# Block exchanges that land on every fourth partition, in a transformer block with expert routing

## The chip, the cores and the metric

The kernel runs on one core of a Trainium2 chip. Its time is the device time of one execution in microseconds (us). Lower is better. It was run three times; the median is what a change is compared with.

## The reference

A transformer block on 16 sequences of 256 tokens, width 256, all in f32:

```python
shift = silu(t) @ W_ada.T + b_ada                  # per sequence
h = ln(x, ln1_g, ln1_b) + shift
qkv = (h @ Wqkv.T).reshape(b, n, 3, 16, 64)        # 16 heads of 64
q = ln(qkv[:, :, 0] per head, qn_g, qn_b)          # normalised over the head's 64 values
k = ln(qkv[:, :, 1] per head, kn_g, kn_b)
attn = softmax(q @ k.T / 8);  x = x + (attn @ v) @ Wout.T
gate = softmax(x @ Wgate.T)                        # 8 experts
vals, idx = top_k(gate.T, 512)                     # each expert takes its 512 best of 4096 tokens
y = (gelu(ln(x[idx]) @ fc1.T + b1) @ fc2.T + b2) * vals
x[idx] += y
```

## The kernel before, in words

**Attention, sequence by sequence.** A sequence's 256 tokens are two tiles (t) of 128. `First` normalises them and transposes them to `hT`. `Group(b, g, t)` multiplies one tile by 512 columns of the qkv weights (g 0 and 1 are queries, 2 and 3 keys, 4 and 5 values), so a group holds eight heads. For queries and keys ScalarE squares the result (L701), VectorE sums each head's 64 squares (L705), GpSimd takes the power -1/2 (L103), and VectorE scales the result into `qk` (L721). The mean over a head needs no instruction there, because the query and key weights are centred once at the start (`center`, L604 and L605). `Quad(b, d)` is four heads: two pairs i, each with two heads j. `scores` (L813) works on a pair with its two heads side by side in TensorE, `maxima` (L821) and `exps` (L830) make the exponentials `pr` and their sums, `normalise` (L841, GpSimd) divides, and `product` (L900) multiplies the transposed probabilities `prT` by the values. `Tail` projects (L926), adds the residual, normalises for the experts and makes the gate's logits.

**Two ways to transpose.** Queries, keys and probabilities have to be transposed, 128 by 128 and f32. For the sequences in `DIRECT` (0 and 15) TensorE does it against an identity matrix (L730 for q and k, L881 for probabilities), and ScalarE copies the result out of PSUM (L742, L888). For the other 14 sequences VectorE transposes inside 32x32 blocks (`turn`, L754 and L851), and an exchange through DRAM puts the blocks where they belong: one store of 512 KB (`away`, L761 and L859) and four loads of 128 KB (`back`, L773 and L873), load q writing the 32 partitions from 32q on. ScalarE then applies the gains to q and k (`affine`, L781 and L789). All these DMAs are issued by SyncE.

**The routing.** As soon as sequences 0 to 14 are done, a search over 30 bits finds for each expert the value of its 256th best gate. Every step is a compare and count on VectorE (L1091), a matmul that adds the counts (L1100) and a decision on VectorE (L1115), one after the other. Sequence 15's attention goes on beside it, and TensorE gets filler transposes (`fill`, L551) where it would sit idle. The routing's first instruction on TensorE is a transpose of the gates (L1028). After the search come a placement, a list of tokens and the first gathers.

**The experts.** Fifteen of the 16 jobs (eight experts, each once for the first 256 tokens and once for the rest) run in a plain loop of `up` (L1286), `gelu`, `down` (L1302) and a scatter, with the second routing's steps spread between them; the first job runs at the end of the planned part.

**What sets the order.** Each engine runs its instructions in the order in which they were issued. For the attention and the first routing, `at(...)` records 3863 steps, and the tuple `PLACES` gives each of them a place; the steps are issued sorted by place. So the order is a written list, and a change of steps needs another list.

Of the kernel before, what the change touches and what calls it, by code (L numbers as in the profile page):

```python
# [12 lines left out]
AF = mybir.ActivationFunctionType  # L13
ALU = mybir.AluOpType
AX = mybir.AxisListType
# [3 lines left out]
P = 128  # L19
# [45 lines left out]
def kernel(  # L65
# [83 lines left out]
    def make_others():  # L149
# [21 lines left out]
    DIRECT = (0, B - 1)  # L171
# [11 lines left out]
        0.3, 0, 3.3, 4.02, 3.75, 5.04, 4.42, 7.26, 0, 0, 8, 9.39, 21.59, 15.62, 11.2, 13.11,  # L183
        17.01, 18.4, 0, 0, 0, 0, 0, 0, 0, 3.5, 4.21, 5.54, 4.52, 5.23, 6.09, 6.6, 7.26, 10.88,
        12.83, 15.02, 15.97, 19.79, 26.15, 26.82, 14.6, 16.55, 20.39, 21.18, 23.31, 28.69, 29.8,
        16.33, 18.28, 20.99, 23.06, 25.36, 27.79, 28.46, 20.58, 22.53, 23.91, 24.94, 27, 28.24,
        29.13, 24.1, 26.05, 33.83, 36.09, 29.35, 31.3, 32.01, 32.8, 34.94, 36.73, 37.55, 31.08,
        33.03, 33.74, 34.68, 36.66, 53.28, 54.22, 37.45, 40.14, 40.85, 42.51, 44.49, 48.92, 51.33,
        39.18, 41.13, 41.84, 44.39, 46.57, 52.83, 53.55, 47.04, 49.88, 49.37, 52, 32.81, 35.54,
        36.58, 38.73, 40.91, 41.63, 34.34, 35.13, 39.64, 41.35, 42.12, 38.46, 43.11, 35.71, 37.26,  # L190
        38.22, 40.69, 41.79, 42.61, 37.86, 39.18, 41.6, 42.67, 44.05, 40.42, 46.02, 47.26, 44.13,
        45.37, 46.16, 50.43, 53.73, 55.38, 45.97, 48.92, 51.34, 54.17, 54.89, 50.16, 57, 45.15,
        47.17, 47.96, 53.16, 63.68, 68.13, 47.77, 50.37, 52.25, 64.12, 67.64, 51.61, 70.34, 71.58,
        55.11, 56.95, 58.1, 60.54, 66.44, 67.15, 56.35, 57.14, 59.63, 78.31, 81.13, 59.36, 83.25,
        56.13, 59.53, 64.4, 68.49, 77.87, 78.83, 58.15, 59.06, 67.58, 80.48, 81.62, 66.42, 84.27,
        86.99, 74.97, 76.5, 77.37, 83.28, 91.94, 92.75, 77.1, 79.32, 82.37, 90.48, 91.2, 80.91,
        94.7, 81.36, 83.07, 83.86, 89.48, 96.74, 97.55, 85.48, 87.48, 90.39, 94.26, 96.51, 89.21,
        101.81, 103.78, 115.15, 119.13, 120.28, 120.28, 121.51, 122.02, 123.82, 124.54, 127.81,
        128.58, 118.62, 122.45, 124.6, 123.6, 124.46, 125.96, 131.29, 132, 134.85, 135.67, 0,
        14.5, 15.21, 24.51, 12.59, 13.3, 22.98, 42.23, 43.1, 51.1, 53.05, 53.76, 54.55, 57.55,  # L200
        58.75, 60.22, 62.17, 62.88, 63.82, 65.82, 66.61, 58.34, 60.44, 61.15, 61.94, 63.92, 65.21,
        66.01, 67.37, 70.57, 72.17, 76.37, 61.95, 63.9, 64.61, 65.7, 67.68, 68.47, 69.27, 70.63,
        73.83, 75.43, 80.28, 64.71, 66.66, 68.61, 70.56, 66.88, 68.83, 69.54, 70.33, 72.31, 73.1,
        71.36, 73.46, 74.17, 74.96, 77.7, 78.49, 73.24, 75.19, 75.9, 76.84, 79.1, 80.3, 81.1,
        82.46, 85.66, 87.26, 91.69, 75.99, 78.33, 79.7, 80.49, 82.47, 83.67, 84.47, 85.83, 89.03,
        90.63, 95.66, 78.75, 82.11, 85.14, 88.44, 82.38, 84.88, 86.03, 87.54, 88.6, 84.28, 85.07,
        88.45, 89.51, 87.27, 90.63, 92.63, 95.83, 97.43, 106.44, 90.92, 92.16, 93.24, 96.03,
        97.14, 92.76, 94.2, 96.94, 98.95, 95.76, 99.75, 101.11, 104.31, 105.91, 111.23, 114.89,
        95.72, 97.75, 98.54, 105.78, 106.84, 98.35, 104.27, 106.69, 108.65, 105.51, 109.45,
        111.11, 114.31, 116.23, 129.4, 100.79, 102.03, 102.82, 107.6, 111.66, 102.63, 105.23,  # L210
        108.51, 112.87, 106.47, 113.67, 115.03, 118.46, 120.66, 130.42, 131.51, 107.46, 109.86,
        111.01, 118.96, 120.13, 109.26, 110.05, 114.35, 118.52, 114.08, 125.1, 127.2, 130.51,
        133.3, 141.66, 108.48, 111.06, 112.93, 115.26, 116.69, 110.46, 111.97, 116.17, 117.3,
        114.85, 118.1, 119.46, 123, 125.2, 140.64, 142.75, 112.25, 115.02, 115.88, 121.61, 127.2,
        114.25, 117.33, 122.52, 129.35, 121.34, 130.15, 132.1, 135.7, 138.5, 144.42, 124.04,
        125.39, 126.18, 128.68, 131.68, 125.99, 127.14, 129.59, 132.81, 128.41, 133.61, 135.3,
        138.5, 140.5, 145.44, 148.04, 162.09, 166.05, 167.29, 167.2, 168.45, 170.6, 176.27,
        177.75, 178.81, 179.57, 165.56, 169.54, 171.6, 170.69, 171.55, 172.1, 179.26, 182.41,
        182.94, 184.62, 0, 25.96, 26.82, 28.77, 24.84, 27.58, 28.44, 80.92, 82.6, 87.02, 88.97,
        90.12, 91.3, 93.36, 94.15, 88.75, 90.7, 91.41, 93.18, 95.16, 96.53, 92.53, 95.16, 95.93,  # L220
        97.85, 99.83, 101.03, 101.83, 103.19, 106.39, 109.11, 113.89, 97.33, 99.5, 100.43, 101.22,
        103.23, 104.02, 105.91, 107.91, 111.11, 112.71, 118.29, 99.06, 106.19, 109.35, 116.84,
        102.83, 107.18, 108.05, 109.42, 112.27, 117.91, 104.71, 106.68, 107.45, 111.3, 113.48,
        123.45, 113.27, 115.38, 116.09, 117.08, 120.74, 121.84, 122.64, 124, 127.2, 128.8, 135.66,
        122.09, 124.04, 124.79, 125.58, 127.81, 128.74, 129.54, 130.9, 134.1, 136.5, 140.7,
        125.93, 129.06, 131.66, 135.17, 125.06, 131.08, 132.3, 134.29, 135.83, 126.59, 128.1,
        135.2, 137.04, 134.02, 137.84, 142.5, 145.7, 147.3, 151.65, 128.38, 130.48, 133.26,
        139.13, 140.19, 133.42, 137.62, 140.04, 142, 138.86, 142.8, 144.16, 147.36, 149.3, 158.17,
        159.41, 133.83, 135.07, 136.66, 141.86, 150.58, 136.44, 138.58, 140.95, 149.36, 139.82,
        151.38, 153.33, 157.29, 160.13, 174.38, 142.53, 144.37, 145.16, 148.86, 159.5, 143.77,  # L230
        146.12, 149.77, 156.32, 148.59, 160.3, 162.13, 165.33, 166.93, 175.4, 177.26, 143.55,
        145.57, 147.08, 156.65, 163.01, 147.38, 151.38, 155.74, 162.23, 152.62, 163.81, 165.73,
        169, 171.33, 188.03, 152.67, 153.91, 154.7, 161.71, 163.62, 156.93, 157.72, 160.8, 164.83,
        159.33, 166.93, 168.93, 172.6, 174.2, 187.01, 190.56, 153.69, 155.11, 160.3, 164.02,
        172.48, 157.53, 161.26, 163.11, 173.09, 162.84, 177.27, 179.47, 183.07, 185.07, 192.51,
        159.19, 160.43, 164.77, 168.87, 178.44, 161.63, 163.81, 167.96, 173.7, 167.65, 179.24,
        180.67, 185.03, 188.27, 193.53, 194.62, 200.92, 204.76, 207.03, 205.96, 207.15, 209.49,
        214.68, 215.39, 217.95, 220.68, 209.17, 212.86, 214.51, 214.65, 215.68, 217.39, 219.42,
        220.01, 224.43, 225.43, 0, 29.62, 30.62, 42.89, 26.48, 29.1, 43.22, 133.39, 134.22,
        135.45, 139.54, 141.4, 142.77, 144.97, 146.17, 137.18, 140.04, 140.8, 144.65, 146.78,  # L240
        147.98, 138.91, 142.19, 142.9, 146.53, 148.76, 149.97, 150.77, 152.13, 155.33, 156.93,
        162.22, 148.19, 150.14, 151.19, 151.98, 154.51, 155.71, 156.93, 158.93, 162.13, 163.73,
        167.93, 146.31, 148.53, 156.44, 158.68, 149.92, 152.34, 153.05, 153.86, 158.73, 165.44,
        154.56, 156.66, 158.13, 158.92, 161.03, 168.93, 160.21, 163.22, 164.23, 165.02, 167.05,
        167.84, 168.64, 170.13, 174.2, 176.2, 181.41, 169.03, 170.98, 171.88, 172.67, 174.91,
        176.11, 176.91, 178.27, 181.47, 183.07, 187.27, 170.76, 172.71, 177.08, 179.96, 172.49,
        175.51, 176.3, 180.52, 181.58, 174.31, 175.1, 181.43, 182.49, 179.73, 184.67, 187.07,
        190.27, 191.87, 198.01, 173.51, 176.72, 180.45, 182.46, 185.39, 177.32, 179, 183.37,
        184.78, 182.19, 187.27, 190.27, 193.47, 195.07, 213.66, 214.9, 185.12, 187.85, 188.64,
        195.66, 196.89, 187.25, 189.6, 194.75, 196.28, 193.28, 198.67, 201.03, 207.89, 210.23,  # L250
        222.54, 186.14, 192.68, 193.47, 196.57, 198.1, 189.06, 191.55, 197.48, 198.71, 194.71,
        199.51, 202.23, 205.43, 207.03, 221.52, 223.68, 199.03, 200.27, 201.06, 205.05, 206.37,
        200.87, 202.02, 204.14, 205.76, 203.87, 207.53, 209.03, 217.89, 220.23, 228.22, 200.05,
        201.47, 202.98, 207.25, 208.71, 202.07, 204.94, 208.16, 209.93, 206.98, 210.73, 212.23,
# [1383 lines left out]
```

## Time and profile before

| | |
|---|---|
| Three runs | 1088.24, 1091.94, 1093.52 us (median 1091.94) |
| Profiled execution | 1091.3 us |
| Its span | 1089.5 us |
| Granted TensorE clock, mean | 0.993 |
| TensorE busy | 1050.4 us, 96% of the span |
| VectorE busy | 809.4 us, 74% |
| GpSimd busy | 617.5 us, 57% |
| ScalarE busy | 592.3 us, 54% |
| DMA | 238.56 MB, mean 219 GB/s |
| Exchange DMAs, issue to landing, median | stores 4.7 (probabilities) and 4.1 us (q, k); loads 4.0 to 4.1 us |

The profile is one execution, taken instruction by instruction. Its time is 1.8 us over its span. A row of a group gives line, engine, operation, output and inputs with their shapes, how often, then busy time, the mean duration of one in ns, and the idle time of the engine ahead of it with what ended that. An f32 matmul of the program is two records in the profile, a transpose is one. Busy time counts overlapping instructions once. The page's rows of digits show 40 equal slices of the span, each digit the busy share in tenths.

### The profile page before, as it was taken

What the parts mean: (1) busy time and instruction counts of PE and PEld (TensorE: products, weight loads), DVE (VectorE), ACT (ScalarE), POOL (GpSimd) and SP (SyncE); (2) the same over time, 40 slices, a digit from 0 to 9 for tenths busy, and PEclk for the clock granted to TensorE, in tenths of its full rate; (3) what the DMA queues carried; (4) which work ended last, traced back from release to release, by engine and by line L of the source; (5) the groups of instructions that cost most, each with busy time, mean ns of one, the idle gap of its engine ahead of it and who ended that gap; (6) DMA issues with size and microseconds to landing.
All of it is one profiled execution on the core that took longest, in us unless ns stands there. A gap on an engine that the chain in (4) does not pass through costs nothing. (4 is left out here: it accounts for less than half of the span.)

```text
span 1089.5 us, 18716 instructions
## 1 busy us (share of the span) xinstructions
PE 1050.4 (96%) x5611; PEld 686.6 (63%) x5611; DVE 809.4 (74%) x2257; ACT 592.3 (54%) x1656; POOL 617.5 (57%) x997
## 2 busy tenths in 40 slices
PE   6999999999999999999999999999988999999996
PEld 4555646555454655555565555656667888888885
DVE  6658888889788797898888887885678588655440
ACT  1768666666566665675666656675612322332331
POOL 3676776778667686667757666665501333333332
PEclk9999999999999999999999999999999999999998
DMA  6025899999999999998999999985130556655661
GB/s 214 1 78 165 269 276 304 291 281 257 283 292 280 280 299 290 289 280 263 277 299 286 265 302 265 321 260 164 61 102 20 149 161 199 186 171 163 192 203 20
DMA packets 167700, 238.56 MB, mean 219 GB/s; under 512 B 17328, under 2 KB 139440, under 8 KB 167600
## 3 DMA queue, kind: packets, MB, share of 16 engines
q1 hardware_dynamic: 159680, 227.08, 69.9%
q0 software_dynamic: 6144, 8.39, 4.2%
q10 hardware_dynamic: 1776, 1.90, 0.5%
q8 instruction: 45, 0.74, 0.3%
q14 instruction: 55, 0.45, 0.1%
HBM read 136.64 MB, written 100.66 MB: 218 GB/s over the span
## 5 line engine op out<-in xcount | busy, mean ns | idle before, releaser
L688 PE MATMUL pm<-wq,hT 128*128 128x512 f32 x768 | 362.1, 607 | 10.1 <-DVE qk L721 3.9
L841 POOL TENSOR_SCALAR pr<-pr,sums 128x256 f32<-128x256 f32 x512 | 237.6, 485 | 102.6 <-DVE sums L837 95.0
L830 ACT ACTIVATE pr<-sc,nmax 128x256 f32<-128x256 f32 x512 | 237.7, 482 | 92.3 <-DVE nmax L821 75.2
L688 PEld LDWEIGHTS pm<-wq,hT 128*128 128x128 f32 x768 | 137.1, 191 | 165.3 <-issue 131.3
L103 POOL TENSOR_TENSOR ss<-ss,neghalf 128x8 f32<-128x8 f32 x128 | 211.2, 1650 | 10.7
L821 DVE TENSOR_REDUCE nmax<-sc 128x2 f32<-128x512 f32 x256 | 165.3, 672 | 19.4 <-PE sc L813 19.1
L851 DVE STREAM_TRANSPOSE pb<-pr 128x512 f32<-128x512 f32 x224 | 150.0, 689 | 15.9 <-POOL pr L841 9.4
L813 PE MATMUL sc<-kT,qT 64*128 64x256 f32 x1024 | 136.8, 396 | 1.0 <-ACT kT L789 0.6
L701 ACT ACTIVATE sq<-pm 128x512 f32<-128x512 f32 x128 | 76.4, 605 | 102.5 <-PE pm L688 100.5
L900 PE MATMUL po<-prT,v 128*64 128x256 f32 x1024 | 129.0, 387 | 1.3 <-DMA prT<-blocks 1.3
L813 PEld LDWEIGHTS sc<-kT,qT 64*128 64x128 f32 x1024 | 91.3, 186 | 50.3 <-issue 28.9
L1319 POOL DMA_INDIRECT out<-y,idx x32 | 51.3, 1604 | 120.6 <-DVE y L1313 66.0
L1286 PE MATMUL ph<-xT,w 128*128 128x256 f32 x512 | 117.8, 383 | 0.0
L1302 PE MATMUL py<-w,hid 128*128 128x256 f32 x512 | 116.3, 380 | 0.0
L926 PE MATMUL pw<-wo,oT 128*128 128x256 f32 x512 | 115.3, 382 | 0.0
L926 PEld LDWEIGHTS pw<-wo,oT 128*128 128x128 f32 x512 | 96.2, 190 | 20.9 <-issue 6.0
L830 ACT ACTIVATION_READ_ACCUMULATOR pr<-sc,nmax 128x1 f32 x512 | 109.2, 213 | 0.0
L900 PEld LDWEIGHTS po<-prT,v 128*64 128x64 f32 x1024 | 66.5, 136 | 66.0 <-issue 20.1
L705 DVE TENSOR_REDUCE ss<-sq 128x8 f32<-128x512 f32 x128 | 85.0, 669 | 28.8 <-ACT sq L701 28.3
L1293 ACT ACTIVATE hid<-ph,vec 128x256 f32<-128x256 f32 x128 | 60.4, 474 | 84.4 <-PE ph L1286 79.4
L1302 PEld LDWEIGHTS py<-w,hid 128*128 128x128 f32 x512 | 95.6, 190 | 12.8
L1286 PEld LDWEIGHTS ph<-xT,w 128*128 128x128 f32 x512 | 95.4, 190 | 12.8
(141 smaller groups left out, 1098.3 us busy)
## 6 DMA issues: line engine op xcount, KB each, us to landing
blocks<-pb SPq DMA_DIRECT2D x112, 512.0 KB, 4.7
prT<-blocks SPq DMA_DIRECT2D x448, 128.0 KB, 4.1
kblocks<-kb SPq DMA_DIRECT2D x56, 512.0 KB, 4.1
w<-in_fc2T SPq DMA_DIRECT2D x16, 1024.0 KB, 5.8
w<-in_fc1T SPq DMA_DIRECT2D x16, 1024.0 KB, 8.3
qraw<-kblocks SPq DMA_DIRECT2D x112, 128.0 KB, 4.0
kT<-kblocks SPq DMA_DIRECT2D x112, 128.0 KB, 4.1
out<-tok SPq DMA_DIRECT2D x32, 128.0 KB, 3.9
```

What stands on the lines that cost most here:

```text
L103: nc.gpsimd.tensor_tensor(dst, src, neghalf[:, : src.shape[1]], ALU.pow)
L688: nc.tensor.matmul(self.pm, hTs[self.b][:, c, bass.ts(self.t, P)], wq[:, c, bass.ts(self.g, GW)], start=(c == 0), stop=(c == DC - 1),)
L705: nc.vector.tensor_reduce(self.ss[:, 0, :], self.sq.rearrange("p (h d) -> p h d", d=HD), AX.X, ALU.add,)
L813: nc.tensor.matmul(self.sc[i, j][:, t, :], qTs[self.b][rows, hp, bass.ts(t, P)], keys[rows, hp] if direct else keys[rows, hp // 4, hp % 4] ...
L821: nc.vector.tensor_reduce(self.nmax[i, j], self.sc[i, j], AX.X, ALU.max, negate=True)
L830: nc.scalar.activation(self.pr[i, j][:, t, :], self.sc[i, j][:, t, :], AF.Exp, bias=self.nmax[i, j][:, t : t + 1], scale=1.0, accum_out=se ...
L841: nc.gpsimd.tensor_scalar(self.pr[i, j][:, t, :], self.pr[i, j][:, t, :], self.sums[i][:, 1, j, t : t + 1], 1.0, ALU.mult, ALU.mult,)
L851: nc.vector.transpose(self.pb[i][:, :, :, j].rearrange("p k c t n -> p t k c n"), self.pr[i, j].rearrange("p t (k c m) -> p t k c m", c=TB ...
L900: nc.tensor.matmul(self.po[j * HD : (j + 1) * HD, i, :], vs[self.b][:, c, bass.ts(4 * self.d + 2 * i + j, HD)], prT[:, j, c] if self.b in ...
L926: nc.tensor.matmul(self.pw, oTs[self.b][:, hp // 2, self.t, hp % 2, :], wo[:, hp, :], start=(hp == 0), stop=(hp == HP - 1),)
L1286: nc.tensor.matmul(self.ph[f], self.w1[:, c, bass.ts(f, P)], self.xT[:, c, :], start=(c == 0), stop=(c == DC - 1),)
L1302: nc.tensor.matmul(self.py[i], self.hid[:, f, bass.ts(i, P)], self.w2[:, f, :], start=(f == 0), stop=(f == FC - 1),)
```

## The change

Four parts, made together.

1. The four loads of an exchange write every fourth partition (q, q+4, q+8, ...) instead of 32 partitions in a row.
2. So that this gives the right rows, queries and keys are laid out by quarter: of a head's 64 values, quarter q holds values q, q+4, q+8, and so on. The host reorders the rows of the query and key weights; centring, statistics, scaling and block transposes follow that layout. Centring becomes three operations (sum, multiply a 128x8 tile by -1/64, add). Sequence 0, which is still transposed by TensorE, is scaled back into the natural order, with a step of four elements in the write. For the probabilities, the exponentials read the scores in PSUM with a step of four elements and write them in a row. Keys are now read in their natural order by the scores.
3. Sequence 15 exchanges its queries, its keys and the probabilities of its first eight heads (d = 0 and 1) too; its last eight heads are still transposed by TensorE. `DIRECT` (q and k by TensorE) is now sequence 0 alone, and `OFFS` lists the quads whose probabilities TensorE transposes.
4. `PLACES` is another list, with 3883 places, so the steps of the attention and of the first routing are issued in another order.

```diff
-    DIRECT = (0, B - 1)
+    DIRECT, OFFS = (0,), {(b, d) for b in (0, B - 1) for d in range(HP // 2)} - {(B - 1, 0), (B - 1, 1)}
     PLACES = (
...
         def center(g, c):
-            w3 = wq[:, c, bass.ts(g, GW)].rearrange("p (h d) -> p h d", d=HD)
+            w3 = wq[:, c, bass.ts(g, GW)].rearrange("p (q e d) -> p q e d", q=QB, e=8)
             ws = stat.tile([P, 8], F32, tag="ws", bufs=2, name="ws")
-            nc.vector.tensor_reduce(ws, w3, AX.X, ALU.add)
-            nc.vector.scalar_tensor_tensor(
-                w3, ws.unsqueeze(2).to_broadcast([P, 8, HD]), -1.0 / HD, w3, ALU.mult, ALU.add
-            )
+            nc.vector.tensor_reduce(ws, w3.rearrange("p q e d -> p e q d"), AX.XY, ALU.add)
+            nc.vector.tensor_scalar_mul(ws, ws, -1.0 / HD)
+            nc.vector.tensor_tensor(w3, w3, by_head(ws), ALU.add)
+
+        def by_head(x):
+            return x.unsqueeze(1).unsqueeze(3).to_broadcast([P, QB, 8, HD // QB])
...
                 nc.vector.tensor_reduce(
-                    self.ss[:, 0, :], self.sq.rearrange("p (h d) -> p h d", d=HD),
-                    AX.X, ALU.add,
+                    self.ss[:, 0, :], self.sq.rearrange("p (q e d) -> p e q d", q=QB, e=8),
+                    AX.XY, ALU.add,
                 )
...
+                if self.b in DIRECT:
+                    dst = self.qk.rearrange("p (e d q) -> p q e d", q=QB, e=8)
+                else:
+                    dst = self.qk.rearrange("p (q e d) -> p q e d", q=QB, e=8)
                 engine.tensor_tensor(
-                    self.qk.rearrange("p (h d) -> p h d", d=HD),
-                    src.rearrange("p (h d) -> p h d", d=HD),
-                    self.ss[:, 1, :].unsqueeze(2).to_broadcast([P, 8, HD]), ALU.mult,
+                    dst, src.rearrange("p (q e d) -> p q e d", q=QB, e=8),
+                    by_head(self.ss[:, 1, :]), ALU.mult,
                 )
...
-                        raw[bass.ts(q, SQ)], self.blocks[:, :, q].rearrange("k d n -> d k n")
+                        raw[q::QB], self.blocks[:, :, q].rearrange("k d n -> d k n")
...
-                keys = plain(kTs[self.b]) if direct else (
-                    kTs[self.b].rearrange("p g k t h m -> p g h (k t) m")
-                )
+                if whole:
+                    keys = plain(kTs[self.b])
+                else:
+                    keys = kTs[self.b].rearrange("p g k t h m -> p g h t k m")
...
+                    dst, src = self.pr[i, j][:, t, :], self.sc[i, j][:, t, :]
+                    if not ((self.b, self.d) in OFFS):
+                        dst = dst.rearrange("p (q c m) -> p q c m", q=QB, c=TB)
+                        src = src.rearrange("p (c m q) -> p q c m", q=QB, c=TB)
                     nc.scalar.activation(
-                        self.pr[i, j][:, t, :], self.sc[i, j][:, t, :], AF.Exp,
+                        dst, src, AF.Exp,
...
-                        prT[bass.ts(q, SQ)], self.blocks[i][:, :, q].rearrange("k m n -> m k n")
+                        prT[q::QB], self.blocks[i][:, :, q].rearrange("k m n -> m k n")
...
+    qk = a["Wqkv"][: 2 * H * HD].reshape(-1, 8, HD // 4, 4, D).transpose(0, 3, 1, 2, 4)
...
-        "wqkvT": a["Wqkv"].T,
+        "wqkvT": np.concatenate([qk.reshape(-1, D), a["Wqkv"][2 * H * HD :]]).T,
```

In `product`, `evict` and the recording of the steps, `b in DIRECT` becomes `(b, d) in OFFS` where probabilities are meant.

## The prediction

> **What bounds the kernel now.** First the slices of the page: TensorE is full nearly everywhere, and the DMA engines are full through the attention.
>
> ```profile
> PE   6999999999999999999999999999988999999996
> ACT  1768666666566665675666656675612322332331
> DMA  6025899999999999998999999985130556655661
> ```
>
> Then the busy time by stage (stretch, its length, busy us and count of PE, PEld, DVE, ACT, POOL, granted clock, DMA share, GB/s): the start, the first sequence, the steady attention, the stretch up to the routing of sequences 0 to 14, that routing, and the experts.
>
> ```profile
> 0.00:27.00 27.00, 18.35 (x56) 11.56 (x56) 16.80 (x35) 4.32 (x7) 8.23 (x20) 0.94 0.65 216
> 27.00:54.00 27.00, 25.19 (x124) 13.87 (x123) 17.65 (x40) 19.21 (x49) 19.07 (x31) 0.99 0.00 1
> 100.00:700.00 600.00, 590.80 (x2840) 334.76 (x2839) 508.10 (x1014) 386.93 (x1145) 417.59 (x721) 1.00 0.97 282
> 740.00:776.00 36.00, 35.91 (x218) 26.17 (x216) 16.76 (x44) 17.65 (x48) 14.64 (x31) 1.00 0.43 136
> 776.00:820.00 44.00, 36.79 (x259) 26.44 (x257) 32.15 (x172) 14.49 (x41) 12.95 (x28) 1.00 0.19 64
> 860.00:1089.00 229.00, 219.74 (x1412) 192.19 (x1410) 130.49 (x710) 67.40 (x140) 74.90 (x57) 0.99 0.55 160
> ```
>
> From 100 to 776 us TensorE is busy 98 to 99% of the time: this stretch ends when its list of matmuls is done. From 776 to 820 it is busy 84% and much of that is filler: there the chain of 30 routing steps between VectorE and TensorE sets the end. The experts are TensorE again. The waits of TensorE say which other engine holds it up: VectorE for q and k in the first sequence, a DMA once.
>
> ```profile
> PE pm L688 <- DVE qk L721: 3.9, 4, 2.9
> PE po L900 <- DMA prT<-blocks: 1.3, 1, 1.3
> ```
>
> So what counts is matmul work ahead of the routing, the length of the routing's chain, and the start. The profiled execution took 1091.3 us (span 1089.5, 1.8 around it), 0.6 below the median of 1091.94; the sum is made against 1091.3. Below 0.5% (5.5 us) a measurement of this kernel can't be told from no change.
>
> **Sequence 15's transposes leave TensorE.** In the built order, TensorE has 32 fewer transposes of q and k (L730) and 32 fewer of probabilities (L881), 16 batches of four, all ahead of the routing's first transpose. The groups, and the timeline of a stretch that shows what one batch costs:
>
> ```profile
> L830 ACT ACTIVATE pr<-sc,nmax 128x256 f32<-128x256 f32 x512 | 237.7, 482 | 92.3 <-DVE nmax L821 75.2 <-POOL pr L841 7.8 <-POOL ss L103 4.8
> L721 DVE TENSOR_TENSOR qk<-pm,ss 128x512 f32<-128x512 f32 x128 | 86.7, 678 | 20.1 <-POOL ss L103 18.3 <-PE pq L730 0.4
> L881 PE MATMUL pp<-ident,pr 128*128 128x128 f32 x128 | 18.9, 278 | 1.6 <-POOL pr L841 1.2
> L730 PE MATMUL pq<-ident,qk 128*128 128x128 f32 x64 | 9.0, 277 | 1.8 <-DVE qk L721 1.8
> ```
>
> ```profile
> 770.67 0.60 PE L730 MATMUL pq<-ident,qk 128*128 128x128 f32 x4
> 771.11 0.60 PE L881 MATMUL pp<-ident,pr 128*128 128x128 f32 x4
> ...
> 779.96 1.14 PE L813 MATMUL sc<-kT,qT 64*128 64x256 f32 x8
> ...
> 781.02 1.08 PE L900 MATMUL po<-prT,v 128*64 128x256 f32 x8
> 781.13 1.29 DVE L821 TENSOR_REDUCE nmax<-sc 128x2 f32<-128x512 f32 x2 [0.19 <-PE sc L813]
> 782.33 0.21 DVE L1115 SCALAR_TENSOR_TENSOR cand<-pc,drop,keep 128x1 f32<-128x1 f32 x1
> ```
>
> Busy time would give 9.0/16 = 0.56 and 18.9/32 = 0.59 us a batch, but the tails overlap: from one batch's start to the next stage's it is 771.11 - 770.67 = 0.44. I take 0.45: 16 x 0.45 = 7.2 us. Against that, the last 8 score matmuls of sequence 15 (16 records, two blocks of 8) now stand ahead of the routing; in the order they are 512 before it instead of 504, so one block's worth of what TensorE still had to do there: 781.02 - 779.96 = 1.06. The order also has 25 fewer changes of kind ahead of the routing, about half of them those batches; a change costs about 0.1 us (four qkv matmul records take 1.81 us to the next stage, eight 3.43), so another 0 to 1.3. Net 6.1 to 7.5; I take **-7.0**. It counts in full, because this stretch has no idle TensorE to lose it in.
>
> **The routing's chain.** Its steps run at 1.00 us where undisturbed (the last fourteen), but seven of 30 take 1.75 to 3.6 us: four behind scores, maxima and products of sequence 15, three behind its projection. Two pairs of maxima (1.29 us each, above) and the scores that feed them leave the chain; the pair at 781.13 makes that step 2.26 us, 1.26 over. The projection stays and only moves later. So 0 to -2.5, **-2.0** taken.
>
> **The start.** Centring a weight group is now three VectorE operations, not two: 8 more of a 128x8 form; the nearest row is a reciprocal on 128x4, 157 ns: 8 x 0.16 = 1.3 us. Sequence 0's eight scalings write q and k with a step of four elements. No row has that; the bounds are the same operation now (0.68) and the one f32 write with a hop for each element: a 224-element product takes 765 ns written across (L998) and 391 written in a row (L990), 1.67 ns an element more, 0.85 us for 512.
>
> ```profile
> L998 DVE TENSOR_TENSOR gate_of<-gates,smax x3: 185/186/765, 757.8 to 854.4; 128x16 f32<-128x16 f32 x2, 128x224 f32<-128x224 f32 x1
> L990 DVE TENSOR_TENSOR gates<-gates,smax x3: 174/175/391, 756.2 to 851.7; 128x16 f32<-128x16 f32 x2, 128x224 f32<-128x224 f32 x1
> ```
>
> That is 0 to 6.8 us of VectorE in the stretch where TensorE waits for exactly these. On the other side the new order puts the first scaling behind five centrings instead of seven, 2 x 1.37 = 2.7 us sooner, of a wait of 2.9 us. Net -1.5 to +6; **+1.5** taken, near the row's half.
> [...]
>
> **Exponentials read PSUM with a step of four.** 464 of 512 do (all but sequence 0's and half of sequence 15's). The trace has no such ScalarE read. Bounds: nothing, and the same 1.67 ns an element: 256 x 1.67 = 0.43 us each on 482 ns. I take 0 on the path, because ScalarE covers it: 613 of 768 qkv records lie in 100 to 700 us, 12.8 sequences of 47.0 us, with 30.3 us of ScalarE each (64%). VectorE stands at 39.8 us (85%) and TensorE is not held up by it. If the cover goes, see the first rival.
>
> **Things with one answer.** The reduction for the statistics and the scaling by quarter read the same number of elements in runs of 16: 0. The query-key and product matmuls read runs of 32 or 64 as before: 0. Sequence 15's exchange adds 8 stores and 32 loads on SyncE's queue (0.43 us an issue, 17 us), 8.4 MB, and 16 VectorE block transposes (0.69 each, 11 us) in 660 to 760 us, and takes 8 evictions (0.80) and 8 copies (0.60) from ScalarE, which gets six other evictions (0.82 to 1.25) instead; VectorE's and the queue's part lies beside TensorE, which has 85% and less around it. Loads to every fourth partition: the same bytes; TensorE waits for such loads 1.3 us in all, so 0.
>
> **Sum:** 1091.3 - 7.0 - 2.0 + 1.5 = 1083.8, **1084 us**; by the parts' ends 1079 to 1089.
>
> **Rivals.**
>
> *ScalarE becomes the limit (slower).* At 0.43 us more for each exponential, 32 a sequence make 13.8 us: 30.3 + 13.8 = 44.1 of 47.0 us, 94%. The pure rate decides only from 0.52 us, but the order is fixed by a list of places, four score tiles are all there are, and each is freed by the exponentials. At 1 to 2 us lost in each of 14 sequences: 1098 to 1112. For it: the only hopping f32 row doubles its time. Against: that row is VectorE's write to SBUF, and ScalarE has a third of its time free. Chance 0.22.
> [...]
>
> *The gain is given back (no change).* TensorE's queue is in order, and two products of sequence 15's first heads, which now wait for an exchange, stand ahead of the routing's transpose, and all the routing behind them. Store to landing is 4.7, four issues 1.7, load to landing 4.1: 10.5 us after the block transposes, and other traffic can add to it; a wait of 3 to 5 us, with the start at its dear end, gives 1088 to 1093. For it: the DMA engines are full up to 740 us. Against: TensorE waited once for such a load. Chance 0.16.
>
> *Loads free more than the sum says.* TensorE is idle 9.2 us in 100 to 700 us; ScalarE waits 12.3 us for keys and 8.9 for queries. If landings shorten and the new order fits them, half to two thirds of the 9.2 goes: 1078. Chance 0.12.
> [...]
>
> **How the numbers follow.** Forecast 0.50, rivals 0.22, 0.16, 0.12. The forecast's own range is 1079 to 1089, and about one eighth of it lies above 1086.5, where 0.5% begins. Faster by over 0.5%: 0.50 x 0.88 + 0.12 = 0.56; within: 0.06 + 0.15 = 0.21; slower: 0.22 and a little of the second rival, 0.23. The range reaches from 1076, below the third rival, to 1102, into the first; what is left out is the rest of the first, some 0.15, and a little below.
>
> **What would show it.** Right: the routing's first transpose starts near 769 instead of 776.6 us, its last step some 9 us sooner; exponentials still near 482 ns; TensorE at 98% from 100 to 700; experts unchanged in length. Wrong: exponentials at 600 ns or more, with TensorE waiting for ScalarE's score tiles; a long wait of a product for its load just ahead of the routing; scalings of sequence 0 at 1.3 us or more, with the first scores later than 36.8 us.

## The result and the profile after

The changed kernel takes 1134.48 us (median of 4 runs, 1132.67 to 1140.39) where the kernel before, on the same chip, takes 1090.55 (4 runs). It is slower: ratio 1.042, 95% interval 1.038 to 1.045. The forecast was 1084, its range ended at 1102. The profiled execution took 1140.4 us (span 1138.6), the longest of the four; in it the loss is 49.1 us of span.

The slices of the page of the changed kernel, to be laid beside those of before: TensorE has eights inside the attention, where it had nines alone, and its dip is longer and lies later; the DMA engines, which stood at 9 through the attention, now stand at 7 and 8.

```profile
PE   7899999999899899999999999989778999999996
ACT  1677665565666475665666566565521432233331
DMA  6025878878877788887888877878803365565661
```

The busy time by stage of the changed kernel (stretch, its length, busy us and count of PE, PEld, DVE, ACT, POOL, granted clock, DMA share, GB/s):

```profile
0.00:27.00 27.00, 19.16 (x57) 11.14 (x58) 18.28 (x41) 4.92 (x8) 9.47 (x22) 0.79 0.66 216
27.00:54.00 27.00, 23.83 (x113) 12.97 (x111) 17.41 (x37) 15.52 (x37) 17.26 (x30) 0.95 0.00 1
100.00:700.00 600.00, 568.17 (x2694) 320.74 (x2694) 478.45 (x959) 367.75 (x1093) 392.76 (x681) 0.99 0.80 266
740.00:776.00 36.00, 32.99 (x152) 17.58 (x151) 27.30 (x53) 24.54 (x74) 22.82 (x38) 0.91 0.76 255
776.00:820.00 44.00, 38.59 (x210) 25.27 (x210) 30.57 (x71) 22.56 (x73) 22.64 (x48) 0.94 0.86 288
```

In 100 to 700 us TensorE is idle 31.8 us where it was 9.2, it got through 2694 matmul records where it was 2840, and every other engine did 5 to 6% less too. The DMA engines moved 266 GB/s instead of 282 with a share of 0.80 instead of 0.97. So every engine waits more, while the DMA engines have more room than before. The stretch from 776 to 820 us, which held the routing before, still holds attention: the routing's first transpose starts at 822.1 us instead of 776.6, 45.5 later. From it to the end of the span it is 316.5 us (312.9 before). So 45.5 of the 49.1 us lie ahead of the routing, in the attention.

The granted clock falls too: in these five stretches it is 0.79, 0.95, 0.99, 0.91 and 0.94, where it was 0.94, 0.99, 1.00, 1.00 and 1.00. Up to the routing's first transpose the trace has TensorE at half clock for 41.0 us, and for 3.4 us in the kernel before. In the steady attention, from 100 to 700 us, three stretches at half clock begin at 292, 391 and 698 us, each within 1 us of the end of an idle gap of TensorE of 1.9 to 3.4 us; one of 2.5 us, from 495.6, has none behind it. So some waits seem to cost more than their own length here; an estimate from all the half-clock stretches is at most 41.0/2 - 3.4/2 = 18.8 us of the 45.5. No run takes the clock apart from the waits.

What holds TensorE up, from its waits in the changed kernel (us in total, times, longest):

```profile
PE po L913 <- DMA prT<-blocks: 11.5, 8, 2.9
PE pm L693 <- DVE qk L730: 6.7, 5, 2.8
```

Products wait for loads 11.5 us (1.3 before). ScalarE's wait for keys went from 12.3 to 30.4 us and for queries from 8.9 to 17.7; the row for keys, of the changed kernel and then of the kernel before:

```profile
ACT kT L797 <- DMA kT<-kblocks: 30.4, 18, 5.0
ACT kT L789 <- DMA kT<-kblocks: 12.3, 13, 1.9
```

And the loads themselves, by line (count, issue time in ns as least/median/most, first and last start):

```profile
L886 SPq DMA_DIRECT2D prT<-blocks x464: 577/602/1882, 99.2 to 825.8; - x155
L781 SPq DMA_DIRECT2D qraw<-kblocks x120: 577/602/1567, 72.7 to 799.6; - x120
```

The same two lines of the kernel before:

```profile
L873 SPq DMA_DIRECT2D prT<-blocks x448: 302/430/2175, 97.3 to 748.8; - x150
L773 SPq DMA_DIRECT2D qraw<-kblocks x112: 302/430/1318, 73.6 to 702.7; - x112
```

Here lies the difference that matters. A load of the same 128 KB now occupies SyncE's queue for 0.60 us instead of 0.43, and never less than 0.58 where the least was 0.30. There are 48 of them in a sequence. The exponentials, which the first rival feared for, did not move (482 ns before):

```profile
L843 ACT ACTIVATE pr<-sc,nmax 128x256 f32<-128x256 f32 x512 | 237.1, 478 | 134.7 <-DVE nmax L830 108.6
```

### The profile page after: what moved, and what is told of

Its sections match the earlier page's. It is cut to its first block, busy times and chain, and to the rows that moved or that the text cites. A ratio compares the mean times of both kernels' runs of the same rounds, so it can differ in the third digit from the quotient of the medians.

```text
span 1138.6 us, 18715 instructions
## 1 busy us (share of the span) xinstructions
PE 1062.9 (93%) x5547; PEld 688.5 (60%) x5547; DVE 821.5 (72%) x2281; ACT 588.1 (52%) x1646; POOL 615.4 (54%) x997
## 5 line engine op out<-in xcount | busy, mean ns | idle before, releaser
L693 PE MATMUL pm<-wq,hT 128*128 128x512 f32 x768 | 369.1, 618 | 17.7 <-DVE qk L730 6.7
L693 PEld LDWEIGHTS pm<-wq,hT 128*128 128x128 f32 x768 | 140.2, 195 | 179.5 <-issue 140.3
L864 DVE STREAM_TRANSPOSE pb<-pr 128x512 f32<-128x512 f32 x232 | 154.3, 688 | 35.7 <-DMA kblocks<-kb 18.0
L822 PE MATMUL sc<-kT,qT 64*128 64x256 f32 x1024 | 142.0, 401 | 5.9 <-ACT pr L843 3.8
L913 PE MATMUL po<-prT,v 128*64 128x256 f32 x1024 | 133.6, 398 | 14.5 <-DMA prT<-blocks 11.5
L822 PEld LDWEIGHTS sc<-kT,qT 64*128 64x128 f32 x1024 | 94.6, 189 | 55.9 <-issue 26.3
L913 PEld LDWEIGHTS po<-prT,v 128*64 128x64 f32 x1024 | 68.8, 140 | 83.2 <-issue 32.7
L730 DVE TENSOR_TENSOR qk<-pm,ss 128x512 f32<-128x512 f32 x128 | 89.7, 702 | 22.9 <-POOL ss L103 20.8
```

The costliest lines, as they stand in the source:

```text
L693: nc.tensor.matmul(self.pm, hTs[self.b][:, c, bass.ts(self.t, P)], wq[:, c, bass.ts(self.g, GW)], start=(c == 0), stop=(c == DC - 1),)
L730: engine.tensor_tensor(dst, src.rearrange("p (q e d) -> p q e d", q=QB, e=8), by_head(self.ss[:, 1, :]), ALU.mult,)
L822: nc.tensor.matmul(self.sc[i, j][:, t, :], qTs[self.b][rows, hp, bass.ts(t, P)], keys[rows, hp] if whole else keys[rows, hp // 4, hp % 4], ...
L864: nc.vector.transpose(self.pb[i][:, :, :, j].rearrange("p k c t n -> p t k c n"), self.pr[i, j].rearrange("p t (k c m) -> p t k c m", c=TB ...
L913: nc.tensor.matmul(self.po[j * HD : (j + 1) * HD, i, :], vs[self.b][:, c, bass.ts(4 * self.d + 2 * i + j, HD)], prT[:, j, c] if (self.b, s ...
```

## The experiments

**Theory 1:** a load that fills every fourth partition takes longer to issue; SyncE's queue issues all loads and stores of the exchanges in order, each behind its own waits, and it became late, so loads, keys and queries arrive late. **Rival 2:** the new order of steps, or sequence 15's exchange, is what costs. **Rival 3:** the layout by quarter, or the reads of PSUM with a step of four, cost. Later a fourth came up, which the expectations call theory 2: what counts is **how long the DMA engines are kept**, not the queue.

### order_alone and loads_alone: the two halves of the change

order_alone is the kernel before with the new places and sequence 15's exchange; loads_alone is the changed kernel with the places of before and sequence 15 on TensorE.

```
order_alone, against before:
-    DIRECT = (0, B - 1)
+    DIRECT, OFFS = (0,), {all quads of 0 and 15} - {(B - 1, 0), (B - 1, 1)}
+    (the new PLACES; transposes and products of sequence 15 by OFFS; its keys read in natural order)
loads_alone, against the changed kernel:
-    DIRECT, OFFS = (0,), {...} - {(B - 1, 0), (B - 1, 1)}
+    DIRECT = (0, B - 1)
+    OFFS = {(b, d) for b in DIRECT for d in range(HP // 2)}
+    (the PLACES of before)
```

> The changed kernel's list of places and its exchange of sequence 15, with the weights, statistics and exponentials of before, and loads that fill 32 neighbouring partitions. Theory 1 (a load to every fourth partition takes 0.60 us to issue on SyncE's queue where the others take 0.43, and that queue is what became late): the gain forecast for the transposes and the routing appears, 1080 to 1086 us, loads issue at 0.43 us median. Rival 2 (the new order or sequence 15's exchange is what costs): 1120 to 1135 us.

> The changed kernel's loads, layout and exponentials with the order of before and sequence 15 transposed on TensorE as before. Theory 1: 1125 to 1145 us, loads issue at 0.60 us, TensorE's busy share from 100 to 700 us falls from 98.5% to about 94%. Rival 2 (the order costs): 1090 to 1095 us.

order_alone: 1101.31 us, ratio 1.0073 (1.0051 to 1.0096). loads_alone: 1132.56 us, ratio 1.0354 (1.0322 to 1.0386). The loads and their layout carry nearly all of the loss, as theory 1 says, and loads_alone lies where theory 1 put it. But order_alone lies in neither of its two ranges: the order alone is not the gain of 8 us that the prediction had, it costs 9. Its waits of TensorE from 700 to 790 us, around the routing's first transpose (782.8 us here), say where a part of that lies:

```profile
PE po L905 <- DMA prT<-blocks: 5.0, 4, 2.7
PE po L905 <- DVE sums L842: 2.0, 1, 2.0
```

And the stage of 760 to 780 us, of order_alone and then of the kernel before:

```profile
760.00:780.00 20.00, 16.10 (x96) 11.83 (x96) 16.12 (x41) 13.60 (x48) 8.97 (x22) 0.96 1.02 325
```

```profile
760.00:780.00 20.00, 19.91 (x144) 15.36 (x140) 9.95 (x34) 11.65 (x37) 7.30 (x19) 1.00 0.24 86
```

Where the DMA engines had come to rest before (0.24), they are now full (1.02) with sequence 15's blocks among others, and products wait for loads. Of the 5.0 us only 1.8 lie ahead of the routing's first transpose, with the 2.0 of the second row; the rest comes behind it. Another part lies earlier: from 100 to 700 us TensorE is idle 14.4 us (600 - 585.62), where it was 9.2.

### step_undone: the destination's step alone

```
-                        raw[q::QB], self.blocks[:, :, q]...
+                        raw[bass.ts(q, SQ)], self.blocks[:, :, q]...
-                        prT[q::QB], self.blocks[i][:, :, q]...
+                        prT[bass.ts(q, SQ)], self.blocks[i][:, :, q]...
```

> The changed kernel with one thing undone: each load fills 32 neighbouring partitions instead of every fourth (so rows of q, k and the probabilities stand in another order and the attention's values are others; every instruction and byte is the same). Theory 1: issue back at 0.43 us, the attention back at 98% of TensorE, 1082 to 1090 us. Rival 3 (the layout by quarter or the reads of PSUM with a step of four cost): it stays at 1125 to 1135 us.

1101.61 us, ratio 1.009 (1.0066 to 1.0113): 33 us better than the changed kernel by this edit alone, and the same as order_alone (1101.31), which has the old layout. So the layout by quarter, the strided reads of PSUM and the longer centring cost together nothing beyond the spread of these runs (1096 to 1106 us for both); rival 3 falls as a cause of the 44 us. Issue and the attention are back where they were, the DMA engines too:

```profile
L886 SPq DMA_DIRECT2D prT<-blocks x464: 302/430/1711, 97.7 to 782.1; - x155
```

```profile
100.00:700.00 600.00, 588.52 (x2833) 334.92 (x2830) 507.42 (x1012) 385.70 (x1140) 418.20 (x721) 1.00 0.97 280
```

Not 1082 to 1090, as expected: the order's 9 us are in it.

### one_load: an exchange with a single load

In the layout by quarter, partition 4d + q wants row (d, q) of the block, so without the spare row one stride describes all 128 rows:

```
-                self.blocks = dram.tile([QB, SQ, QB + 1, N], ...)
+                self.blocks = dram.tile([QB, SQ, QB, N], ...)
-                for q in range(QB):
-                    nc.sync.dma_start(raw[q::QB], self.blocks[:, :, q].rearrange("k d n -> d k n"))
+                nc.sync.dma_start(raw, self.blocks.rearrange("k d q n -> (d q) k n"))
                 (and the same for prT)
```

> The changed kernel with each exchange's four loads of 128 KB to every fourth partition replaced by one load of 512 KB to all 128 partitions (the spare row of the DRAM block goes too, so that the source is one stride). The bytes are the same. If the count of issues on SyncE's queue is what is late: 12 issues of 0.4 to 0.6 us a sequence instead of 48 of 0.6, so the queue is idle most of the time and the time falls to 1076 to 1086 us. [...]

1074.34 us, ratio 0.9833 (0.9805 to 0.986): 60 us faster than the changed kernel and 17.5 faster than the one before. It beats both, and is 2 us better than the range expected. The loads' issue and the steady attention:

```profile
L882 SPq DMA_DIRECT2D prT<-blocks x116: 359/371/1457, 99.9 to 759.8; - x116
```

```profile
100.00:700.00 600.00, 599.47 (x2918) 344.13 (x2918) 519.52 (x1038) 399.98 (x1181) 427.56 (x737) 1.00 0.85 289
```

TensorE is idle half a microsecond in 600, and the DMA engines move more (289 GB/s) at a lower share (0.85). Several things changed at once here: the issues on the queue, the partitions that one load reaches, and the spare row of the block in DRAM. The next two, both without the spare row, take the first two apart.

### by_key_block and by_half: issues against DMA engines

```
by_key_block: for k in range(QB): nc.sync.dma_start(raw[:, k], self.blocks[k].rearrange("d q n -> (d q) n"))
by_half:      for r in (slice(0, 64), slice(64, 128)): nc.sync.dma_start(raw[r], src[r])
```

> The changed kernel with four loads of 128 KB for each exchange again, but each fills all 128 neighbouring partitions with one of the four key blocks, instead of every fourth partition with all four. As many issues as the changed kernel, the same 1 KB packets, all partitions reached by each load. If the 0.60 us issue comes from the step of four, these issue at 0.43 us or less. Theory 2 (the DMA engines, which were busy at 0.97 to 1.02 with loads to 32 neighbours and 0.85 with one load to 128, are what limits): 1073 to 1080 us, DMA share near 0.85. Theory 1 (the count of issues on SyncE's queue alone): 1095 to 1103 us like step_undone, whose issues are as many and as long.

> The changed kernel with two loads of 256 KB for each exchange, one to partitions 0 to 63 and one to 64 to 127. Half the issues of the changed kernel, at 0.35 to 0.45 us. Theory 1 (issues): close to one_load, 1073 to 1080 us. Theory 2 (a load that reaches only a part of the partitions keeps the DMA engines longer): DMA share 0.95 or more from 100 to 700 us and 1090 to 1101 us.

by_key_block: 1083.09 us, ratio 0.9916 (0.99 to 0.9933).

```profile
L884 SPq DMA_DIRECT2D prT<-blocks x464: 319/430/1985, 100.2 to 771.7; - x155
```

```profile
100.00:700.00 600.00, 594.73 (x2885) 340.37 (x2884) 514.84 (x1028) 394.79 (x1174) 424.29 (x732) 1.00 0.86 286
```

by_half: 1103.94 us, ratio 1.0107 (1.009 to 1.0123).

```profile
L886 SPq DMA_DIRECT2D prT<-blocks x232: 573/608/1396, 99.6 to 787.4; - x116
```

```profile
100.00:700.00 600.00, 584.59 (x2811) 330.87 (x2811) 501.75 (x1003) 385.62 (x1141) 415.73 (x717) 1.00 0.98 278
```

by_key_block lies between the two ranges expected of it. by_half's issues took 0.61 us, not 0.35 to 0.45, and its time lies 3 us above the range of theory 2. Both theories are true, each in its place. by_key_block has as many issues as step_undone, as long (0.43), and is 18 us faster: what the traces show to differ is the DMA share, 0.86 against 0.97. by_half has half the issues and is no faster than step_undone: its DMA share is 0.98, though the spare row is gone. So with loads that fill 32 or 64 neighbours the DMA engines were full (0.97 and 0.98), and that was a limit of the kernel before. The trace's packets of 1 KB, nine in ten of them those of the exchanges' loads, say the same: from 100 to 700 us one kept its DMA engine for 66 ns on average in the kernel before, 67 in step_undone and 69 in by_half, but 54 in the changed kernel, 53 in by_key_block and 52 in one_load.

Between by_key_block (0.43 us an issue) and the changed kernel (0.60), with as many issues and both DMA shares low (0.86, 0.80), lie 51 us. That points to the queue, and so do the 9 us from by_key_block to one_load; some_issues and more_issues, below, test it.

### one_load_old_order: the order, where loads are no limit

```
one_load with DIRECT = (0, B - 1), OFFS = all their quads, and the PLACES of before
```

> One load for each exchange in the layout by quarter, with the list of places of before and sequence 15 transposed on TensorE. Beside one_load (1074 us) it prices the new order and sequence 15's exchange where loads are no limit: by the prediction's terms (7.0 for the transposes, 2.0 for the routing) 1081 to 1085 us. If the order is worth nothing or harms, as order_alone suggests with its +9 us: 1064 to 1075 us.

1081.02 us, ratio 0.9903 (0.9887 to 0.992), within the interval expected. So the order and sequence 15's exchange are worth 1081.0 - 1074.3 = 6.7 us once the loads are cheap. With order_alone and loads_alone this makes a table of medians:

| loads | order of before | new order | the order's price |
|---|---|---|---|
| to 32 neighbours, 0.43 us | 1091.9 (before) | 1101.3 (order_alone) | +9.4 |
| to every fourth, 0.60 us | 1132.6 (loads_alone) | 1134.5 (changed kernel) | +1.9 |
| one to all 128, 0.37 us | 1081.0 | 1074.3 (one_load) | -6.7 |

The +1.9 is within the spread of its runs (1129 to 1133 and 1133 to 1140 us, measured at different times), so there the order's price can't be told from nothing.

### step_two: does the step's size matter?

```
+    raw[64 * (q // 2) + q % 2 : 64 * (q // 2) + 64 : 2]   (and prT)
```

> The changed kernel with loads to every second partition (32 partitions within 64, so rows stand in another order and the attention's values are others). It asks whether the issue time grows with the step or jumps as soon as partitions aren't neighbours. If it jumps: 0.60 us median and 1125 to 1140 us. If it grows with the step: 0.48 to 0.55 us and 1100 to 1125 us. If only a step of four is dear: 0.43 us and 1095 to 1103 us.

1141.24 us, ratio 1.047 (1.0429 to 1.0511), 1 us above the range for a jump. The issue time jumps:

```profile
L886 SPq DMA_DIRECT2D prT<-blocks x464: 571/602/1660, 98.7 to 825.1; - x155
```

A step of two costs as much as a step of four. But it isn't the step alone: by_half's loads to 64 neighbours have the same floor, 0.573. Nor is the step without effect: in more_issues, below, loads of 4 bytes to 16 partitions take 0.492 us at least with a step of four and 0.338 to neighbours. What makes 32 neighbours (0.302) and 128 (0.319 with one key block, 0.359 with four) cheap stays open.

### some_issues and more_issues: the queue alone

one_load, with small loads behind each exchange's load, which carry hardly any bytes and which nothing reads:

```
+        def at(rows): c = next(spares) % 64; return spare[rows, c : c + 1], vecs[rows, 0:1]
+        nc.sync.dma_start(*at(slice(0, P, 4)))      # both
+        nc.sync.dma_start(*at(slice(0, 64, 4)))     # more_issues only
+        nc.sync.dma_start(*at(slice(64, P, 4)))     # more_issues only
+        nc.sync.dma_start(*at(slice(0, 16)))        # both
```

> one_load with two loads of 4 bytes a partition behind each exchange's load, into a spare tile: one to every fourth partition, one to 16 neighbours. It adds issues to SyncE's queue and hardly any bytes. At 0.58 and 0.35 us they make 11 us a sequence, so the queue's issues of exchanges come to some 20 us a sequence: between one_load's 8 (1074 us) and by_key_block's 25 (1083 us). Theory 1 (issue time on the queue): 1076 to 1084 us. If only the landing of strided blocks were dear: 1073 to 1076 us.

> The same with four such loads (three to every fourth partition, one to 16 neighbours): 25 us of issues more a sequence, 33 in all, near the changed kernel's 35, while the blocks still arrive by one load to neighbours and the DMA engines stay below 0.95. Theory 1: 1105 to 1135 us, TensorE waiting for loads and ScalarE for keys and queries as in the changed kernel. If what costs is not the issue but the landing of blocks spread over every fourth partition: 1073 to 1085 us.

some_issues: 1079.65 us, ratio 0.9883 (0.9855 to 0.9912). more_issues: 1172.42 us, ratio 1.0732 (1.07 to 1.0763). The first lies within its range, the second 37 us above the range of theory 1, on the side of theory 1. The attention and the waits of more_issues:

```profile
100.00:700.00 600.00, 554.07 (x2576) 309.66 (x2575) 461.95 (x924) 351.97 (x1043) 381.01 (x659) 0.97 0.78 253
```

```profile
PE po L921 <- DMA prT<-blocks: 18.0, 11, 4.4
ACT kT L807 <- DMA kT<-kblocks: 33.6, 17, 5.0
```

Its blocks still arrive by the loads of the fastest kernel, and its DMA engines are at 0.78. Only the queue is fuller, and the picture of the changed kernel comes back, stronger: products and keys wait, 98 us are lost on one_load. Slower landings are not the cause. Matching the trace's packets to the DMAs in the order of their issue gives an estimate of when the last byte of a load of probabilities lands: at the median 3.6 us after its issue here and 4.1 in one_load, 2.1 in the changed kernel and 2.5 in the kernel before. So loads arrive late because they are issued late, and a full queue alone does this. Why it costs more than expected is not taken apart; the half clock is a part of it (30.7 us of it from 100 to 700 us, 11.7 in the changed kernel, none in one_load). The next table sets the kernels side by side. Issue per sequence is worked out from the medians by line: 12 exchanges with one store each, and the loads; the queue's idle time is the sum of all waits of SyncE's queue from 100 to 700 us.

| kernel | issue per sequence, us | queue idle in 600 us | DMA share | median us |
|---|---|---|---|---|
| one_load | 12 x 0.37 + 12 x 0.33 = 8.4 | 442.8 | 0.85 | 1074 |
| some_issues | 12 x (0.37 + 1.15) + 12 x 0.36 = 22.6 | 222.7 | 0.87 | 1080 |
| by_key_block | 48 x 0.43 + 12 x 0.37 = 25.1 | 169.9 | 0.86 | 1083 |
| changed kernel | 48 x 0.60 + 12 x 0.535 = 35 | 125.9 | 0.80 | 1134 |
| more_issues | 12 x (0.38 + 2.34) + 12 x 0.38 = 37 | 79.4 | 0.78 | 1172 |
| by_half | 24 x 0.61 + 12 x 0.39 = 19 | 316.4 | 0.98 | 1104 |
| step_undone | 48 x 0.43 + 12 x 0.36 = 25 | 195.5 | 0.97 | 1102 |

Of the upper five, whose DMA engines have room, the time goes with the issue per sequence, with a bend between 25 and 35 us. A sequence takes some 47. The queue never runs out of idle time, for it issues in the order of the list and waits at a load whose store has not landed, or at a store that VectorE has not made ready. Of the 125.9 us of the changed kernel, 24.9 and 16.1 are waits of loads for a store to land, and 14.1 and 8.8 waits of stores for VectorE's block transposes.

### last_one_load: why the order costs where the DMA engines are full

step_undone, with sequence 15 alone loading by one load to all partitions:

```
+                if self.b == B - 1:
+                    nc.sync.dma_start(raw, self.blocks.rearrange("k d q n -> (d q) k n"))
-                for q in range(QB):
+                for q in range(QB * (self.b < B - 1)):
```

> step_undone (all loads to 32 neighbours, so sequences 1 to 14 give other values) with sequence 15 alone loading each exchange by one load to all 128 partitions. It asks why the new order, worth -7 us where the DMA engines have room, costs +9 where they are full. If it is sequence 15's own exchange, arriving late in front of the routing: the waits of products for loads just ahead of the routing go, and the time falls by 4 to 7 us from step_undone's 1101.6, to 1094 to 1098. If it is the order in the middle sequences: 1099 to 1103 us, with TensorE's idle time from 100 to 700 us as in step_undone (11.5 us).

1096.15 us, ratio 1.0055 (1.0033 to 1.0076): 5.5 better than step_undone by the medians and within what was expected. By the ratios to the kernel before, measured beside each, it is 0.35%, 3.8 us, and the two intervals overlap. The waits of products from 700 to 800 us did not go; they went from 6.8 us to 3.8, and ahead of the routing's first transpose from 3.8 to 1.6:

```profile
PE po L923 <- DMA prT<-blocks: 3.8, 4, 1.7
```

So sequence 15's own exchange, in front of the routing, is perhaps a quarter to a third of the 16 us between the order's price at full DMA engines (+9.4) and at free ones (-6.7); that is a hint, not shown. The rest is not taken apart: sequences 13 and 14 still load the old way here, next to sequence 15, and the DMA share stays at 1.00 from 740 to 776 us.

## Why the prediction was wrong, step by step

**The step that failed** is the half sentence "Loads to every fourth partition: the same bytes; TensorE waits for such loads 1.3 us in all, so 0", together with "0.43 us an issue" for sequence 15's exchange. It took the issue time of a load from a row of loads to 32 neighbours and carried it over to another form, without bounds, although no row of the trace showed that form. It measured 0.60. The price of the mistake is changed kernel minus step_undone: 1134.5 - 1101.6 = 33 us, net of what the DMA engines gained; beside by_key_block, whose engines have the same room, it is 51. And it read "who waits for loads" where it should have asked how full the queue is that issues them: 48 x 0.17 + 12 x 0.16 = 10 us more a sequence, on a queue that was idle 198.6 of 600 us, 15.6 a sequence, all of it waits for something that wasn't ready. What makes the issue of such a load dear stays open.

The sum's own ends were also added wrongly: 1091.3 - 7.5 - 2.5 - 1.5 = 1080 and 1091.3 - 6.1 + 6 = 1091, not 1079 and 1089. That does not reach the 1134 either. That the time came out slower, as the first rival had it, is no credit to that rival: its mechanism did not happen.

**Sequence 15's transposes (-7.0) and its exchange beside TensorE (0).** The first was of the right size only where the DMA engines have room: from one_load_old_order to one_load the routing's first transpose comes 765.9 - 759.7 = 6.2 us sooner, 1.5 of it from the start (first scores 39.0 and 37.5 us), so some 4.7 against 7.0, by one execution of each. The second was wrong where they have none. The profile of before showed them at 0.97 from 100 to 700 us; the 8.4 MB at the 282 GB/s that they moved there are 30 us of a full resource, and the prediction counted the queue's and VectorE's time for them but not that. With loads to 32 neighbours the whole order came out at +9.4 us.

**The routing's chain (-2.0).** From its first transpose to the start of the last of its 30 scans: 42.1 us before, 45.3 in the changed kernel, 41.6 in one_load, 42.2 in one_load_old_order. At best -0.6.

**The start (+1.5).** First scores at 36.8 us before and 37.4 after: +0.6, too little to confirm the term. Kernels with the same start have them from 35.7 (step_undone) over 36.9 (last_one_load) to 37.5 (one_load), in one execution each. loads_alone, with the old order, has them at 38.9 (+2.1) and order_alone at 35.6 (-1.2), in the direction of the two parts. Sequence 0's eight scalings with a step of four, from 15 to 60 us, of the changed kernel:

```profile
L730 DVE TENSOR_TENSOR qk<-pm,ss x8: 1043/1055/1147, 20.7 to 52.8; 128x512 f32<-128x512 f32 x8
```

That is 1055 - 681 = 0.37 us more each; the row's half was 0.43.

**Exponentials (0), reductions, matmul reads (0).** Right within the spread of the runs: 478 against 482 ns, and step_undone equals order_alone (1101.6 and 1101.3). The first rival, 0.22, is refuted: the time came out on its side of no change, by another mechanism and beyond its 1112.

**The second rival** (two products of sequence 15 wait for their exchange in front of the routing) happens. In the changed kernel's timeline, 5 us ahead of the routing's first transpose:

```profile
816.84 1.97 PE L913 MATMUL po<-prT,v 128*64 128x256 f32 x8 [2.93 <-DMA prT<-blocks]
```

It is the longest wait for a load ahead of the routing in step_undone too (3.1 us); in the changed kernel it is a small part of 45 us.

**The third rival** (loads free more) was right in its mechanism and unpaid in the changed kernel. Landings shortened, as it supposed (the 2.5 and 2.1 us above), and the DMA share fell from 0.97 to 0.80; the same step that freed the engines filled the queue. With one load in place of four, the idle time of TensorE from 100 to 700 us goes from 9.2 to 0.5 us, and with the order's gain this is the 1074 us of one_load, below the 1078 that the rival gave.

## What to carry to other kernels

A DMA had two prices here, the time that its engines are kept and the time that its issue takes on SyncE's queue, and both depended on the form of the destination: a change that was free in bytes lowered one (66 to 54 ns a packet) and raised the other (0.43 to 0.60 us). Before a form of transfer is called free, add up the issues of a steady period on its queue, and see what share of the period the queue can spare for its waits. Here a layout that lets four transfers become one was worth more than one that spreads each of them: 1074 against 1134 us.

## What the runs showed of the hardware that was not expected

- Issue on SyncE's queue by form, for the loads of probabilities (least and median ns): 32 neighbouring partitions of four blocks 302 and 430; every fourth 577 and 602; every second 571 and 602; 64 neighbours 573 and 608; 128 neighbours of one block 319 and 430; of four blocks, 512 KB, 359 and 371. At the median one load of 512 KB took less to issue, 371 ns, than any form of 128 KB, 430 to 602.
- In more_issues a load of 4 bytes to every fourth partition, 32 in all, took 495 ns at least to issue and 584 at the median, one to 16 neighbours 338 and 577. The issue of one form varied too: a store of the exchange took 332 at the median in one_load, 376 in more_issues and 535 in the changed kernel, with the same least, 319.
- With loads to every second of 64 partitions (step_two) the DMA share was 0.83 at 266 GB/s; 32 neighbours had 0.97 at 280 (step_undone). Beside the changed kernel, as late and at the same 266 GB/s, it is 0.83 against 0.80, and 58 against 54 ns a packet of 1 KB, not 67 as with 32 neighbours; why loads to 32 neighbours keep the DMA engines longer stays open.
